# A recommender's lookup kernel whose TensorE signals its readers with a drain behind the matmul in place of the matmul itself

## The chip, the cores and the metric

The kernel runs on one core of a Trainium2 chip. The metric is device time in microseconds (us) of that core from start to end of one launch. A core has five engines that run side by side and meet only through semaphores: TensorE (PE in the profile; its weight loads are listed as PEld), VectorE (DVE), ScalarE (ACT), GpSimd (POOL) and SyncE (SP, which here only issues transfers). Matmul results go into PSUM, from which DVE and ACT read them.

## The reference

For each of 16384 rows, tables are looked up and averaged, and a small network runs over the result:

```python
tok = word_emb[token_idx].mean(axis=1)          # 32 rows of 300 floats, 50000-row table
e1 = emb_mh1[mh1_idx].mean(axis=1)              # 20 rows of 64 each, three tables
...
o1 = emb_oh1[oh1_idx]                           # one row of 64, four tables
...
emb = jnp.concatenate([tok, e1, e2, e3, o1, o2, o3, o4], axis=1)
wide = (wide_mh1[mh1_idx].sum(axis=(1, 2)) + ... + wide_oh4[oh4_idx][:, 0])[:, None]
h = jax.nn.relu(emb @ W1 + b1)                  # 748 -> 1024
h = jax.nn.relu(h @ W2 + b2)                    # -> 512
h = jax.nn.relu(h @ W3 + b3)                    # -> 256
return jax.nn.sigmoid(h @ Wd + bd + wide)
```

## The kernel before

The 16384 rows are worked through in 128 tiles of 128 rows. The large table is gathered: for each tile and each of its 32 tokens, POOL issues one indirect DMA of 128 rows of 300 floats into `tok_rows` (`gather`, L238 to L249), and DVE adds them up in `own`, a PSUM bank (`add_up`, L545). The ring `tok_rows` has three buffers of two gathers each, so up to six gathers are outstanding before POOL must wait for DVE.

The small tables are not gathered. They lie on chip as bf16 terms (`terms`), and their lookups are turned into matmuls in two moves. First, how often each table row occurs in a lookup is counted: DVE compares keys with a running index and writes one-hot rows into `hot` (`one_hots`, L619; two buffers), ACT scales half of them in place, TensorE multiplies them into a PSUM bank `pc` (`counts`, L636; two banks), and ACT copies the counts to `cnt`. Each tile takes 11 such steps of up to six matmuls, so there are 128 x 11 = 1408 steps. Second, TensorE multiplies the counts of the tile before with `terms` into the one PSUM bank `pg` (`small_sums`, L659), 138 matmuls a tile in four groups, and DVE reduces each group into the features `g`, 128 x 4 = 512 reductions. As `pg` has no second bank, the next group starts when the reduction is done.

Once features of a few tiles (four, at the end two and one) are complete, they are transposed by TensorE into `pc`, scaled by DVE into `x`, and the network's layers run in f32 (`layer`, L782): matmuls into one of two banks `ph`, each output read by ACT into `odd` or `even`.

The order of work on each engine is written by the main loop (`for step in range(n_steps)`, L948): in each step one-hots for the step after, this step's `pc` matmuls, a share of the `pg` matmuls, token gathers and adds by a pace, and a share of the layers' matmuls. So TensorE's queue holds, in turn, short bf16 matmuls for `pc` and `pg` and long f32 ones for `ph`.

A recording layer sets the waits. Every operation is recorded with what it reads and writes (`Program.record`); where another engine's operation must come first, that one is marked `signals` (L205), and only marked operations increment their engine's semaphore. Operations of TensorE never wait for TensorE. `Program.emit` (L251) then issues everything in the recorded order. All engine operations are issued from the call on L98, so nearly all rows of the profile carry that line, and tile names tell them apart. On TensorE the marked operation is the last matmul of a group whose PSUM bank is read next, or whose operands are overwritten next.

Of the kernel before, what the change touches and what calls it, by code (L numbers as in the profile page):

```python
# [71 lines left out]
class Instruction:  # L72
# [3 lines left out]
    def __init__(self, emit, sequencer, stream):  # L76
        self.emit, self.sequencer, self.stream = emit, sequencer, stream
        self.signals = False
        self.batch = [self]
# [24 lines left out]
class Program:  # L104
# [54 lines left out]
    def covers(one, other):  # L159
        return not one[0] or one[0] == other[0] and one[1] <= other[1] and other[2] <= one[2]  # L160

    def record(self, emit, sequencer, stream, reads, writes, clear=(), batch=None):
        ins = Instruction(emit, sequencer, self.stream(stream))
        if batch is not None:
# [86 lines left out]
    def emit(self, last):  # L251
        semaphores = {}
        counts = [0] * len(self.in_order)

        def semaphore(s):
            if s not in semaphores:
                name = next(n for n, k in self.streams.items() if k == s)
                semaphores[s] = self.tc.alloc_semaphore(f"sem_{name}")
            return semaphores[s]

        for s, ordered in enumerate(self.in_order):
            if any(not ordered or i.signals for i in self.members[s]):
                semaphore(s)

        def wait(engine, waits):
            for k in range(0, len(waits), 2):
                ins = engine.wait_ge(semaphore(waits[k].stream), waits[k].value)
                for o in waits[k + 1 : k + 2]:
                    ins.wait_op(semaphore(o.stream), o.value, "sem-ge")

        with self.tc.tile_critical():
            for ins in self.program:
                engine, waits = self.engines[ins.sequencer], ins.waits
                wait(engine, waits[1:])
                made = ins.emit()
                for o in waits[:1]:
                    made.wait_op(semaphore(o.stream), o.value, "sem-ge")
                s = ins.stream
                if not self.in_order[s]:
                    counts[s] += 16  # L280
                    made.then_inc(semaphore(s), 16)
                elif ins.signals:
                    counts[s] += 1
                    made.then_inc(semaphore(s), 1)
                ins.value = counts[s]
                assert counts[s] < 32768
            wait(self.engines["SP"], last)
# [13 lines left out]
class Banks:  # L301
# [8 lines left out]
    def next(self):  # L310
        if not self.free:
            self.flush()
        bank = self.free.pop(0)
        self.program.taken[bank.tensor.name] = (self, bank)
        return bank
# [756 lines left out]
```

## Time and profile before

| what | value |
|---|---|
| median of 2 runs | 6938.59 us (6930.11 to 6947.07) |
| the profiled execution, span from first to last instruction | 6960.3 us |
| ACT busy / DVE busy / POOL busy | 39% / 51% / 56% |
| TensorE busy | 79% |
| mean granted TensorE clock | 0.882 |
| mean DMA rate | 94 GB/s |
| gathers | 4096, 629.41 MB in 196608 packets |

The profile was taken of one further execution; its span is 21.7 us above the median of the two timed runs. Starts of matmuls in it are recorded, their ends are modelled. A wait is put down to the instruction whose semaphore update came last; "issue" is idle time in which an engine waited for nothing that the profile shows, and "remote" a release for which no instruction that updates that semaphore ended shortly before. A row of the timeline has start, length, engine, line, operation, tiles and count, and in brackets the idle time ahead of it and what ended that.

### The profile page before, as it was taken

To read this page: it belongs to the slowest core of one execution; us is meant where nothing else is said; L and a number is where in the kernel's file an instruction comes from. 1 tells how busy PE (TensorE), PEld (TensorE's weight loads), DVE (VectorE), ACT (ScalarE), POOL (GpSimd) and SP (SyncE) were. 2 spreads that over 40 slices of the span, in tenths; PEclk is the share of its full clock that TensorE was granted. 3 is DMA by queue.
4 is the path that set the end of the run, shared out by engine and by line. 5 is a ranking of instruction groups with operands and counts; after the bars stand their busy time and mean duration, and the time that the engine had idled before them with its cause. 6 is when DMAs were issued, how large, how long until landed. Compare 5 with 4: busy or idle time off the path is not lost.

```text
span 6960.3 us, 83647 instructions
## 1 busy us (share of the span) xinstructions
PE 5506.1 (79%) x33626; PEld 3546.0 (51%) x33626; DVE 3573.8 (51%) x6612; ACT 2697.5 (39%) x3433; POOL 3880.1 (56%) x4103
## 2 busy tenths in 40 slices
PE   5588878788788788887888787887778887878887
PEld 3455455455455545554555555544444554545666
DVE  4555555555555555555555555555555555555441
ACT  4343433333333343343343343333333333434331
POOL 6555555555555555555555555555555555555553
PEclk8788988988888998889889888898888988988898
DMA  5333333333333333333333333333333333333331
GB/s 157 95 93 94 94 94 93 92 95 93 93 96 93 94 93 93 93 95 94 93 94 94 92 94 92 95 90 90 94 92 92 92 94 92 94 92 93 89 92 50
DMA packets 253069, 651.40 MB, mean 94 GB/s; under 512 B 119195, under 2 KB 119835, under 8 KB 252679
## 3 DMA queue, kind: packets, MB, share of 16 engines
q0 software_dynamic: 196608, 629.41, 33.0%
q1 hardware_dynamic: 56071, 16.65, 1.0%
q8 instruction: 262, 4.29, 0.2%
q14 instruction: 128, 1.05, 0.0%
HBM read 645.59 MB, written 0.07 MB: 93 GB/s over the span
## 4 chain that ended last, share of the span: by engine, by line
PE 45%; another core or an unknown queue 19%; DVE 16%; issue 13%; ACT 3%; DMA 2%; POOL 2%; DVEq 0%; ACTq 0%; SPq 0%
PE ph L98 22%; PE pg L98 16%; DVE own L98 8%; PE pc L98 7%; DVE hot L98 6%; DMA tok_rows<-in_word_emb_dram,it 2%; DVE g L98 2%; POOL tok_rows L242 2%; ACT hot L98 1%; ACT cnt L98 1%; DVE x L98 0%; ACT odd L98 0%; ACT terms L98 0%; DVE wide L98 0%
## 5 line engine op out<-in xcount | busy, mean ns | idle before, releaser
L242 POOL DMA_INDIRECT tok_rows<-in_word_emb_dram,it x4096 | 3879.2, 947 | 2999.6 <-DVE own L98 1887.7
L98 PE MATMUL pg<-terms,cnt 128*128 128x195 bf16 x17664 | 2051.5, 267 | 966.2 <-DVE g L98 532.1
L98 PEld LDWEIGHTS pg<-terms,cnt 128*128 128x128 fp8e3 x17664 | 1656.3, 105 | 1229.3 <-DVE g L98 620.2
L98 DVE TENSOR_TENSOR own<-own,tok_rows 128x300 f32<-128x300 f32 x3712 | 1764.4, 475 | 477.6 <-DMA tok_rows<-in_word_emb_dram,it 363.5
L98 ACT ACTIVATE cnt<-pc 128x828 uint16<-128x828 f32 (+1 forms) x1408 | 1187.7, 844 | 2010.6 <-remote 1107.4
L98 DVE TENSOR_TENSOR hot<-own,sc 128x1656 bf16<-128x1656 bf16 (+1 forms) x1408 | 1388.4, 986 | 814.0 <-remote 474.2
L98 ACT ACTIVATE hot<-hot 64x768 bf16<-64x768 bf16 (+1 forms) x1408 | 1155.2, 820 | 1638.9 <-DVE hot L98 1434.6
L98 PE MATMUL ph<-x,w_sb 128*128 128x512 f32 (+5 forms) x3492 | 1604.8, 591 | 65.6 <-issue 43.6
L98 PEld LDWEIGHTS pc<-hot 128*128 128x128 bf16 x8192 | 630.4, 103 | 1025.6 <-issue 784.4
L98 PE MATMUL ph<-odd,w_sb 128*128 128x512 f32 (+2 forms) x2368 | 1088.6, 588 | 54.4 <-issue 51.3
L98 DVE TENSOR_REDUCE g<-pg 128x130 f32<-128x390 f32 (+1 forms) x512 | 260.7, 509 | 1469.1 <-remote 921.2
L98 PE MATMUL pc<-hot 128*128 128x138 bf16 x8192 | 804.3, 234 | 249.8 <-issue 115.1
L98 PEld LDWEIGHTS ph<-x,w_sb 128*128 128x128 f32 (+1 forms) x3492 | 639.6, 207 | 513.3 <-issue 477.4
L98 PEld LDWEIGHTS ph<-odd,w_sb 128*128 128x128 f32 x2368 | 427.9, 207 | 335.0 <-issue 324.6
L98 ACT ACTIVATE odd<-ph,b_sb 128x512 f32<-128x512 f32 (+2 forms) x365 | 231.1, 633 | 206.8 <-remote 91.7
L98 PE MATMUL ph<-even,w_sb 128*128 128x512 f32 (+2 forms) x592 | 278.3, 601 | 8.8 <-issue 8.6
L98 DVE COPY sc<-pc 128x512 bf16<-128x512 bf16 x64 | 44.2, 690 | 343.6 <-PE pc L98 191.7
L98 DVE TENSOR_TENSOR x<-pc,scale 128x768 f32<-128x768 f32 x127 | 120.7, 950 | 155.4 <-PE pc L98 84.5
L98 ACT ACTIVATE even<-ph,b_sb 128x512 f32<-128x512 f32 (+2 forms) x148 | 93.2, 630 | 224.5 <-remote 113.2
L98 PEld LDWEIGHTS ph<-even,w_sb 128*128 128x128 f32 x592 | 111.5, 211 | 92.8 <-issue 87.0
L98 PE MATMUL pc<-ident,g 128*128 128x128 f32 x762 | 115.4, 289 | 45.3 <-ACT cnt L98 26.7
L98 PEld LDWEIGHTS pc<-ident,g 128*128 128x128 f32 x762 | 87.8, 148 | 54.5 <-ACT cnt L98 31.1
(50 smaller groups left out, 547.9 us busy)
## 6 DMA issues: line engine op xcount, KB each, us to landing
tok_rows<-in_word_emb_dram,it POOLq DMA_INDIRECT x4096
ix<-in_idx_dram SPq DMA_DIRECT2D x64, 64.0 KB
w_sb<-in_W_dram SPq DMA_DIRECT2D x6, 512.0 KB
it<-in_idx_dram SPq DMA_DIRECT2D x64, 32.0 KB
w_sb<-in_W_dram SPq DMA_DIRECT2D x1, 2048.0 KB
odd<-in_mh_dram SPq DMA_DIRECT2D x3, 682.5 KB
even<-in_mh_dram SPq DMA_DIRECT2D x1, 682.5 KB
out_dram<-x SPq DMA_DIRECT2D x29, 2.0 KB
```

Source lines behind the costliest of these rows:

```text
L98: lambda: call(*args, **operands), self.name, self.name, aps + list(named.values()), outs
L242: return self.nc.gpsimd.indirect_dma_start(out=out, out_offset=None, in_=table, in_offset=bass.IndirectOffsetOnAxis(ap=index, axis=0),)
```

## The change

Where an operation of TensorE is marked as one that others wait for, `emit` now issues a further instruction of TensorE, a drain, behind it, and hangs the increment on the drain. The matmul itself no longer updates a semaphore. Values, waits and the order of all other instructions stay; on the other engines nothing differs.

```diff
@@ -281,6 +281,8 @@
                     made.then_inc(semaphore(s), 16)
                 elif ins.signals:
                     counts[s] += 1
+                    if ins.sequencer == "PE":
+                        made = self.nc.tensor.drain()
                     made.then_inc(semaphore(s), 1)
                 ins.value = counts[s]
                 assert counts[s] < 32768
```

The wait of the marked matmul was set before this point, so it stays on the matmul. Line numbers of what follows L283 rise by two.

## The prediction

> **What bounds the kernel now.** I read the page first (engines, slices, the chain that ended last), then the view of all instructions of line 98, where every operation is recorded, with the causes that ended its idle time, then the list of waits, then the timeline at two places.
>
> ```profile
> PE 5506.1 (79%) x33626; PEld 3546.0 (51%) x33626; DVE 3573.8 (51%) x6612; ACT 2697.5 (39%) x3433; POOL 3880.1 (56%) x4103
> DMA  5333333333333333333333333333333333333331
> PE 45%; another core or an unknown queue 19%; DVE 16%; issue 13%; ACT 3%; DMA 2%; POOL 2%; DVEq 0%; ACTq 0%; SPq 0%
> ```
>
> TensorE (PE) is busy 5506 of 6960 us, so it stands idle for 1454 us. The chain gives 45% of the span to PE and 19%, 0.19 x 6960 = 1322 us, to "another core or an unknown queue", though the program has one core. Which waits are those?
>
> ```profile
>   remote: 3010.1, 531
> ...
> ACT cnt L98 <- remote: 1107.4, 198, 10.3
> DVE g L98 <- remote: 921.2, 146, 7.4
> DVE hot L98 <- remote: 474.2, 101, 7.9
> ```
>
> The columns are total us and times, and in the last three rows the longest. Waits called "remote" sum to 3010 us in 531 pieces, 5.7 us each. The tiles that carry them are read out of PSUM banks that only TensorE writes (cnt<-pc, g<-pg), or wait for TensorE to be done with a buffer (hot). The view puts down a release as remote where no updating instruction ended shortly before it. So they look like increments of TensorE's semaphore that come long after the matmul. The clearest place is near the end:
>
> ```profile
> 6853.31 0.94 POOL L242 DMA_INDIRECT tok_rows<-in_word_emb_dram,it  x1 [18.84 <-DVE own L98]
> 6856.93 0.37 ACT L98 ACTIVATE odd<-ph,b_sb 128x128 f32<-128x128 f32 x1 [1.70 <-PE ph L98]
> 6860.45 0.37 ACT L98 ACTIVATE odd<-ph,b_sb 128x128 f32<-128x128 f32 x1 [3.16 <-remote]
> 6860.88 2.27 PE L98 MATMUL ph<-odd,w_sb 128*128 128x128 f32 x18 [1.08 <-ACT odd L98]
> 6879.56 0.95 POOL L242 DMA_INDIRECT tok_rows<-in_word_emb_dram,it  x1 [0.30 <-issue]
> 6881.70 0.37 ACT L98 ACTIVATE even<-ph,b_sb 128x128 f32<-128x128 f32 x1 [20.88 <-remote]
> 6882.12 1.22 PE L98 MATMUL ph<-odd,w_sb 128*128 128x128 f32 x4 [18.97 <-issue]
> ```
>
> The 18 matmuls from 6860.88 are through at 6863.15 by the profile. The ScalarE read that waits for the first layer output among them starts at 6881.70, and PE stands idle 18.97 us for that. In between nothing runs but POOL's gathers of token rows, every 1.25 us until 6879.56, and VectorE's adds of those rows. The signal comes about 1.2 us after the last gather instruction ended (6880.51). The reads at the start of that burst, up to 6856.93, were still prompt. So the trace says: while gathers stream, TensorE's completions are told late, and they come when the stream pauses. Two windows of the middle show what else happens then:
>
> ```profile
> 2995.00:3005.00 10.00, 10.00 (x80) 7.22 (x79) 4.96 (x11) 3.42 (x4) 6.80 (x8) 0.97 0.40 108
> 3020.00:3027.00 7.00, 0.73 (x8) 0.49 (x5) 0.45 (x2) 0.16 (x1) 3.49 (x4) 0.71 0.39 111
> ```
>
> Columns: length, busy us (and instructions) of PE, PEld, DVE, ACT, POOL, then clock, DMA share, GB/s. In the first window PE works through; in the second PE, DVE and ACT do next to nothing for 7 us with gathers under way. PE is the bound while it has work, and late completions are the bound when it has run out. Being told late does not stop PE at once: it goes on with whatever waits for nobody. That run-ahead is what the change touches.
>
> **The change, part by part.** The increment is taken off the matmul and put on a drain behind it; no other instruction moves. The PSUM tiles' readers give the number of drains: one signalling matmul for each.
>
> ```profile
> L98 ACT ACTIVATE cnt<-pc x1408: 621/861/902, 8.8 to 6758.7; 128x828 uint16<-128x828 f32 x160, 128x552 uint16<-128x552 f32 x16
> L98 DVE TENSOR_REDUCE g<-pg x512: 349/562/567, 85.1 to 6815.3; 128x130 f32<-128x390 f32 x128, 128x65 f32<-128x195 f32 x43
> L98 ACT ACTIVATE odd<-ph,b_sb 128x512 f32<-128x512 f32 (+2 forms) x365 | 231.1, 633 | 206.8 <-remote 91.7 <-PE ph L98 81.5 <-PE pg L98 16.9
> ```
>
> 1408 + 512 + 365 are three of the groups; the others (even 148, x 127 + 2 + 37, sc 64, terms 40, odd from pc and pg 5) bring 423, together 2708 drains, 1.9 in each of the kernel's 1408 steps. The trace of before has no drain of this sort, so its price is bounded.
>
> First price, the refill. Today the next matmul enters while the signalling one is still in the array; behind a drain it can't. How much overlap is lost is read from merged rows:
>
> ```profile
> 2996.33 0.53 PE L98 MATMUL pc<-hot 128*128 128x138 bf16 x6
> 2996.69 1.63 PE L98 MATMUL pg<-terms,cnt 128*128 128x195 bf16 x17
> 2984.68 1.02 PE L98 MATMUL ph<-odd,w_sb 128*128 128x512 f32 x2 [0.31 <-issue]
> L98 PE MATMUL pc<-hot x8192: 220/223/322, 7.9 to 6758.4; 128*128 128x138 bf16 x200
> L98 PE MATMUL pg<-terms,cnt x17664: 244/248/373, 82.4 to 6815.0; 128*128 128x195 bf16 x199
> L98 PE MATMUL ph<-odd,w_sb x2368: 275/592/1220, 420.1 to 6952.3; 128*128 128x512 f32 x155, 128*128 128x128 f32 x22, 128*128 128x256 f32 x21
> L98 PEld LDWEIGHTS pc<-hot x8192: 95/97/207, 7.9 to 6758.3; 128*128 128x128 bf16 x200
> L98 PEld LDWEIGHTS ph<-odd,w_sb x2368: 186/190/338, 420.0 to 6952.2; 128*128 128x128 f32 x198
> ```
>
> (minimum, median, maximum ns in the last five.) Six pc matmuls take 0.53 us and one 0.223, so they start (0.53 - 0.223) / 5 = 0.061 apart: each overlaps the next by 0.162. For pg it is 0.248 - (1.63 - 0.248) / 16 = 0.162, for the layers 0.592 - (1.02 - 0.592) = 0.164. At least 0.162 us is lost a drain; at most also the weight load that is hidden today, 0.097 for the 1920 drains of pc and pg and 0.190 for the other 788, so 0.29 in the mean. I take the middle, 0.23. It counts where PE had something to go on with: its matmuls wait for another engine some 310 times (179 for DVE g, 78 for ACT cnt, 34 for ACT hot, a few others), so 2708 - 310 = 2398 drains x 0.23 = 551 us (388 to 695).
>
> The TensorE page of the Trainium skill ("TensorE: Matmul & The Clock Gate", step-by-step section) says a lone matmul can't hide the emptying of the array while a stream of them does, some 166 ns at full clock. By that, 2398 x 0.166 = 398 us, an estimate; the rows' 0.162 agrees, without the reload.
>
> Second price, the run-ahead. If the drain waits until the late completions are in, PE stands still for each signal that is late, where today it works on.
>
> ```profile
> PE pg L98 <- DVE g L98: 532.1, 179, 7.9
> PE pc L98 <- ACT cnt L98: 122.9, 78, 7.4
> PE pc L98 <- ACT hot L98: 38.4, 34, 3.2
> ```
>
> Remote waits come to 3010 us on two engines and PE idles for 1454, most of it behind those same waits (532 + 123 + 38 in the rows above, and issue). So at most 3010 - 1454 = 1556 us of PE's work is done today inside them (less where DVE and ACT wait at the same time), and would be pushed out behind them. At the least it is nothing, or negative, if lateness shrinks. It should shrink: PE puts no further instructions behind an untold one, and a signal early in a burst of gathers is prompt (6856.93 above), the later one not. Between all of it and none of it I take half, 1505 us, as PE idle time. The burst above supports it no closer than that: four reads were prompt, two were late.
>
> What then still keeps PE idle without lateness: 179 waits for the reduce x 0.51 us (the page's mean) = 91 us.
>
> Sum against the profiled span: 5506 busy + 1505 late + 551 refill + 91 = 7653 us. The span of 6960.3 is 22 us above the median of the two runs, 6938.6, so 7630 us is forecast, 10% slower. Off PE the change costs nothing: POOL's gathers need 4096 x 1.25 = 5120 us, DVE 3574, ACT 2697, all with room; a drain's own message adds to the wait of each reader, but a reader that waits late already waits for microseconds.
>
> **Rivals.** (a) The drain is told at once. The drain's increment comes from the sequencer and might not stand in whatever queue holds the matmuls' completions. Then lateness is gone: 5506 + 551 + 91 - 22 = 6126 us; by the chain, 6939 - 1322 + 551 = 6168. About 6150 us, faster by 11%. For it: VectorE's adds and semaphores go on undisturbed in the burst above, so it is TensorE's path alone that is held. Against it: a drain that is to mean anything must see the matmuls complete, and what is held looks like the completion. It decides where less than (6939 - 6126) / 3010 = 27% of the lateness stays.
>
> The PSUM page of the skill ("PSUM — Partial Sum Buffer", engine vs sequencer instructions) wants the increment on the matmul, since that fires at completion, and says that a drain waits for the engine to be fully idle. By the first half of that rule nothing is late today but the work itself; by the second the drain inherits the delay, as in my forecast. This trace shows a matmul's message 18 us after its modelled end, which the first half does not lead one to expect.
>
> (b) All lateness stays, each piece now with PE idle: 5506 + 3010 + 695 + 91 - 22 = 9280 us. For it: the 18.97 us above, where nothing but the end of the gathers brought release. Against: early signals of a burst are prompt.
>
> (c) It cancels: lateness falls to about 27%, and refills eat the gain: 6800 to 7077 us.
>
> **How the numbers follow.** The forecast (30 to 80% of the lateness stays, 7029 to 8534 us) gets 0.58, (b) 0.14, (c) 0.10, (a) 0.18. About 2% is what a measurement of this kernel can tell from no change. Slower by over 2%: 0.58 + 0.14 = 0.72; within 2%: 0.10; faster: 0.18. The range goes from the lower edge of (c), 6800, to just over (b), 9300, and leaves out (a) and little else; the forecast's own is 7029 to 8534.
>
> **What would show it.** In the profile after: PE's busy time about as before, its idle time up from 1454 to over 2000 us; remote waits of ACT and DVE replaced by waits on PE's sequencer or on drains; after each signal at least 0.16 us more between matmuls; no PE work inside a late wait. If (a) is right, the 19% of the chain goes to nearly nothing and PE's busy share rises towards 90%. I am wrong if TensorE's signals become prompt while gathers stream, or if the refill is several times 0.23 us because a drain itself takes long.

## The result, and the profile after

| | kernel before | changed kernel |
|---|---|---|
| median of 2 runs | 6938.59 us | 7715.26 us (7701.54 to 7728.99) |
| profiled execution: span | 6960.3 us | 7727.1 us |

The changed kernel is slower by a ratio of 1.1115 (95% interval 1.1088 to 1.1142), 777 us. The forecast was 7630 us.

Here are the engines, and the chain that ended last by engine, from the page of the changed kernel:

```profile
PE 5804.2 (75%) x33626; PEld 3547.7 (46%) x33626; DVE 3610.5 (47%) x6612; ACT 2716.9 (35%) x3433; POOL 3890.1 (50%) x4103
issue 46%; PEld 33%; PEldq 11%; DVE 6%; ACT 3%; DMA 0%; SPq 0%; POOL 0%; DVEq 0%
```

"PEldq" is TensorE's sequencer, where drains are listed. The "another core or an unknown queue" of before is gone from the chain, but not the time: TensorE idles 7727 - 5804 = 1923 us, where it was 1454. From the view of line 98, with the causes that ended idle time, and from the view of the drains' own line 285:

```profile
  PEq L285: 6874.7, 2332
...
L285 PEldq DRAIN  x2709: 13/2272/19290, 4.9 to 7721.6; - x194
```

The first of these rows says that other engines stood 6875 us, in 2332 waits, until a drain ended; there is no "remote" row left. The second gives minimum, median and maximum ns of a drain, from when the sequencer reaches it until it is done, so most of it is the time of matmuls ahead of it that are still to be done. Who stands there is in the view of waits of the changed kernel (us in total, times, longest us):

```profile
POOL tok_rows L242 <- DVE own L98: 2571.9, 936, 19.4
ACT cnt L98 <- PEq L285: 2389.3, 974, 9.6
DVE g L98 <- PEq L285: 1782.4, 385, 10.1
...
DVE hot L98 <- PEq L285: 1154.8, 492, 9.6
...
ACT even L98 <- PEq L285: 281.8, 105, 19.4
```

The readers of all three kinds of PSUM tile (`cnt` from `pc`, `g` from `pg`, `even` from `ph`) wait for drains, and POOL, which issues the gathers, waits for VectorE behind them: every engine is behind TensorE.

What counts is how long a drain goes on behind the modelled end of its last matmul. Taken from the trace for all 2709: 2034 end within 0.15 us of it, most of them 0.021 us behind, and 675 are late, with 1668 us in sum. One of these is in the timeline of the changed kernel:

```profile
3006.60 0.53 PE L98 MATMUL pc<-hot 128*128 128x138 bf16 x6
3007.30 1.55 PE L98 MATMUL pg<-terms,cnt 128*128 128x195 bf16 x16 [0.18 <-issue]
3010.20 0.56 DVE L98 TENSOR_REDUCE g<-pg 128x130 f32<-128x390 f32 x1 [4.67 <-PEq L285]
3010.22 1.12 PE L98 MATMUL ph<-x,w_sb 128*128 128x512 f32 x2 [1.37 <-issue]
```

The pg matmuls end at 3008.85. The reduction that waits for their drain starts at 3010.20, and so does TensorE's next matmul, which waits for nobody but the drain. Before, TensorE would have gone on at once. The 0.18 us ahead of the pg row is a drain that isn't late, seen as a gap between two matmul groups: it ends 0.117 us behind its matmul, and the next matmul starts 0.059 us later.

### The profile page after: what moved, and what is told of

Same layout as the page of the kernel before. It is cut to its first block, busy times and chain, and to the rows that moved or that the text cites. A ratio compares the mean times of both kernels' runs of the same rounds, so it can differ in the third digit from the quotient of the medians.

```text
span 7727.1 us, 86356 instructions
## 1 busy us (share of the span) xinstructions
PE 5804.2 (75%) x33626; PEld 3547.7 (46%) x33626; DVE 3610.5 (47%) x6612; ACT 2716.9 (35%) x3433; POOL 3890.1 (50%) x4103
## 4 chain that ended last, share of the span: by engine, by line
issue 46%; PEld 33%; PEldq 11%; DVE 6%; ACT 3%; DMA 0%; SPq 0%; POOL 0%; DVEq 0%
PEld pg L98 16%; PEldq L285 11%; PEld ph L98 10%; PEld pc L98 7%; DVE hot L98 3%; ACT hot L98 2%; DVE own L98 2%; ACT cnt L98 0%; DVE g L98 0%; SPq L238 0%; DMA tok_rows<-in_word_emb_dram,it 0%; POOL tok_rows L242 0%; ACT x L98 0%; DMA it<-in_idx_dram 0%; DVE x L98 0%
## 5 line engine op out<-in xcount | busy, mean ns | idle before, releaser
L98 PE MATMUL pg<-terms,cnt 128*128 128x195 bf16 x17664 | 2021.1, 273 | 1216.1 <-issue 1144.4
L98 PE MATMUL ph<-x,w_sb 128*128 128x512 f32 (+5 forms) x3492 | 1638.1, 594 | 203.9 <-issue 159.4
L98 PEld LDWEIGHTS pc<-hot 128*128 128x128 bf16 x8192 | 596.9, 101 | 999.2 <-issue 883.2
L98 PEld LDWEIGHTS ph<-x,w_sb 128*128 128x128 f32 (+1 forms) x3492 | 618.5, 204 | 762.9 <-issue 741.7
L98 PE MATMUL pc<-hot 128*128 128x138 bf16 x8192 | 762.6, 230 | 211.5 <-issue 166.9
```

Source lines behind the costliest of these rows:

```text
L98: lambda: call(*args, **operands), self.name, self.name, aps + list(named.values()), outs
```

## The experiments

There are twelve experiments, in four sets, and each set also timed the kernel before. It took 5212 to 5225 us there, not 6939: something about the first pair of runs was different, and it was not the kernel. Comparisons below are within a set where nothing else is said.

**The kernel before, unchanged, for its trace.** No edit.

> The kernel before, unchanged, for a trace under the conditions of the study. If its time is about 5225 us: remote waits below 100 us (3010 us in the first trace), TensorE busy above 90% of the span. Ratio 1.00.

Measured: 5212.61 us, ratio 1.0 (0.9991 to 1.001). From its page, the engines and the chain that ended last:

```profile
PE 4861.1 (93%) x33626; PEld 3267.3 (63%) x33626; DVE 3577.5 (69%) x6612; ACT 2685.7 (52%) x3433; POOL 3875.1 (74%) x4103
POOL 32%; DMA 31%; issue 15%; DVE 14%; PE 8%; ACT 0%; DVEq 0%; POOLq 0%; SPq 0%
```

No wait at all is put down as remote. Of 358 waits that an update of TensorE's semaphore ended, each ended 16 ns or less behind the matmul's modelled end; in the first trace it was 1444 waits with a median of 2273 ns. Of the 1750 us between the two spans, 1105 are idle time of TensorE and 645 are busy time. And the bound is another one: POOL and the DMA of the gathers carry 63% of the chain, TensorE 8%. The view of waits of this run names the same:

```profile
DVE own L98 <- DMA tok_rows<-in_word_emb_dram,it: 1395.3, 1385, 6.7
POOL tok_rows L242 <- issue: 773.5, 2522, 2.0
POOL tok_rows L242 <- DVE own L98: 464.5, 1457, 4.0
```

VectorE stands 1395 us until gathered rows have landed, and POOL waits only 465 us for VectorE to free a buffer, so the gathers are late and not their readers.

**The changed kernel, twice more.** No edit.

> The changed kernel once more, beside the kernel before, since in the first runs of the study the kernel before took 5225 us in place of 6939. If late completions are a condition of where or when a kernel runs, and the refill is a cost of the drain itself: where the kernel before takes about 5225 us, the changed kernel takes 5600 to 5700 us (ratio 1.07 to 1.09), and where it takes about 6940, 7715 (ratio 1.11). If the increment on the drain has a cost of its own beside the drain's stop: above 5750 us.

> The changed kernel a third time, to see whether the conditions of the first pair (kernel before at 6939 us, late completions) come back. Theory: ratio 1.11 if the kernel before takes about 6940 us, 1.07 if it takes about 5215, whatever else differs. If the ratio of 1.11 appeared at 5215 us as well, lateness would not be what separates the two.

Measured: 5581.83 us, ratio 1.0706 (1.0688 to 1.0724), and 5582.75 us, ratio 1.071 (1.0692 to 1.0728). Of 2709 drains none ended more than 0.15 us behind its matmul. The engines and the chain of the first of the two, from its page:

```profile
PE 5266.0 (94%) x33626; PEld 3224.8 (58%) x33626; DVE 3604.5 (65%) x6612; ACT 2707.7 (49%) x3433; POOL 3877.9 (70%) x4103
...
PEld 36%; issue 30%; PEldq 12%; DVE 11%; DMA 4%; POOL 3%; ACT 3%; DVEq 0%; SPq 0%
```

POOL and DMA have 7% of the chain in place of 63%: TensorE's queue (weight loads, their issue, the drains) has become the longest path. TensorE's busy time is up from 4861 to 5266 us, and its idle time is down from 349 to 313 us. The time of the first repetition is 18 us under the 5600 us that its expectation began at; the ratio is inside. So the change loses 7% without any lateness, and 11% with it. The conditions of the first pair did not come back.

**Drain and signal taken apart**, twice.

The cut is against the kernel before.

```diff
                     counts[s] += 1
                     made.then_inc(semaphore(s), 1)
+                    if ins.sequencer == "PE":
+                        self.nc.tensor.drain()
```

> The drain stands behind each signalling matmul, but the increment stays on the matmul, so a reader need not wait for the drain's own message. Theory (TensorE stands still at each drain until its completions are in): the same time as the changed kernel, 7600 to 7800 us. Rival (readers are told later because the message comes from the drain and not from the matmul): near the time of before, 6900 to 7050 us.

> The drain behind each signalling matmul with the increment left on the matmul, once more, beside the changed kernel in the same runs. Theory: within 1.5% of it at about 5215 us for the kernel before (5641 against 5582 was measured in different runs: 1.1% more), and also where completions are late, since TensorE stands still in both. If it is over 2% faster than the changed kernel where completions are late, the readers gain by hearing from the matmul.

Measured: 5641.18 us, ratio 1.0794 (1.0776 to 1.0812), and 5641.12 us, ratio 1.0823 (1.0805 to 1.0841), against 5582.75 us for the changed kernel in the set of the second. The times in us of the first expectation rested on 6939 us for the kernel before and can't be met; as ratios they come to 1.095 to 1.124 for the theory and at most 1.016 for the rival, and 1.079 is in neither. What holds is the comparison with the changed kernel, within the 1.5% of the second expectation. With readers told by the matmul, the whole loss stays, so where completions are prompt it comes from TensorE's stop and not from where the message is sent. It is even 58 us more: these drains end 0.047 us behind the matmul in place of 0.021, and 2709 x 0.026 = 70 us. Whether readers gain by the matmul's message where completions are late wasn't seen.

**The gathers left out, without and with drains.** The adds read zeroed buffers; the token part of the features is left out.

```diff
-                    program.gather(f"gather{tokp.slot}", rows[-1], word, it[:, j : j + 1], batch, tok_rows)
...
+    for rows in tokp.all:
+        nc.vector.memset(rows, 0.0)
```

> The kernel before without the 4096 gathers of token rows (the adds read buffers that are zeroed once; the token part of the features is left out). Theory (TensorE's completions are told late only while gathers stream): remote waits all but gone, TensorE the bound, 5550 to 5900 us. Rival (completions are late by TensorE's own load): remote waits stay in the thousands of us, time above 6500.

> The changed kernel without the gathers, as in the run before it. Theory: the drains then cost the refill alone, 450 to 650 us above the same kernel without drains, and drains that end more than 0.15 us behind their matmul sum to less than 100 us (1668 us with gathers). Rival (a drain is slow by itself): the difference is above 800 us.

Measured: 4810.86 us and 5529.8 us, one run each. The engines of the one, then of the other, from their pages:

```profile
PE 4740.6 (99%) x33626; PEld 3251.6 (68%) x33626; DVE 3563.4 (74%) x6615; ACT 2697.6 (56%) x3433; POOL 0.9 (0%) x7
```

```profile
PE 5256.5 (95%) x33626; PEld 3218.5 (58%) x33626; DVE 3594.6 (65%) x6615; ACT 2710.6 (49%) x3433; POOL 0.9 (0%) x7
```

The first expectation failed on its time, 739 us under its lowest: it reckoned from the first pair. No wait is put down as remote and TensorE is the bound, as it said. It is in both runs, so the difference is the bare price of the drains: 719 us, 0.265 us each. It lies about half way between the theory's upper bound (650) and the rival's lower one (800), so both failed. TensorE's busy time grows by 516 us, 0.190 a drain: matmuls that overlapped now stand one behind the other. Compared matmul by matmul, the two traces give the parts: the signalling matmul overlapped the next one by 423 us in sum, 0.156 each, and with drains by nothing; and the matmul behind a drain takes 97 us longer in sum, 0.036 each, most where it is an f32 one. The TensorE page of the Trainium skill ("TensorE: Matmul & The Clock Gate", step-by-step section) says that a lone matmul can't hide the emptying of the array and a stream does; its section "Single matmul latency" puts at 166 ns what a lone matmul at full clock pays beside its columns, issue included. The 0.156 agrees with that, but as ends of matmuls are modelled, this split rests on the model; the 0.265 us in sum is measured time. TensorE's idle time grows by 203 us, 0.075 a drain, of which the trace shows two parts: the drain ends 0.021 us behind the matmul's modelled end, and the next instruction starts 0.052 us later. That gathers are what makes completions late is not shown by this pair, because in the same set completions were prompt with gathers too.

**Two drains in place of one.**

```diff
+                        self.nc.tensor.drain()
                         made = self.nc.tensor.drain()
```

> The changed kernel with a second drain behind each drain (2709 more); the second finds TensorE empty. Theory (what a drain costs is the emptied array and the restart, not the instruction): 0.01 to 0.06 us for each further drain, 30 to 160 us above the changed kernel (5582 us where the kernel before takes 5214), so 5610 to 5740 us. Rival (a drain costs its 0.265 us as an instruction): 700 us more, near 6300.

Measured: 5782.26 us, ratio 1.1068 (1.105 to 1.1086). Against 5582 us, in another set, that is 200 us for 2709 further drains, 0.074 us each. It is just outside the expected 0.01 to 0.06 us, far from the rival's 0.265, and the same as the 0.075 us above. So a drain costs 0.075 us as an instruction, and 0.19 us because matmuls no longer overlap across it.

**Drains behind some of the matmuls only.** The cut is against the changed kernel; an operation also keeps the name of the tile that it writes.

```diff
-                    if ins.sequencer == "PE":
+                    if ins.sequencer == "PE" and ins.tile.startswith("pc"):
```

> Drains behind the 1604 signalling matmuls that write pc alone; the other 1105 signal by themselves. Theory (each drain costs the same refill wherever it stands): 1604 / 2709 = 59% of the changed kernel's loss, ratio 1.040 to 1.055. Rival (what counts is run-ahead, which TensorE has most of behind the pc matmuls): over 80% of the loss, ratio above 1.063.

> The complement: drains behind the 1105 signalling matmuls that write pg or ph. Theory: 41% of the loss, ratio 1.025 to 1.040, and the losses of this kernel and of the one with drains behind pc alone add up to that of the changed kernel within 60 us. Rival: under 20% of the loss, ratio below 1.016.

Measured: 5285.68 us, ratio 1.0136 (1.0119 to 1.0153), and, with `not` ahead of the second condition, 5227.76 us, ratio 1.0025 (1.0015 to 1.0035). Together they lose 72 + 14 = 86 us, and both at once lose 368. The theory fails in both, and so does the rival of the first; the second lies below its rival's bound of 1.016, but not for its reason. The loss is neither shared by number nor lies behind the pc matmuls. The chains that ended last, first of the kernel with drains behind pc, then of the other, give the reason:

```profile
PE 77%; issue 6%; DVE 6%; DMA 4%; POOL 4%; PEld 2%; PEldq 1%; ACT 0%; DVEq 0%; SPq 0%
```

```profile
DMA 23%; POOL 23%; PE 19%; issue 14%; DVE 12%; PEld 7%; PEldq 1%; ACT 1%; DVEq 0%; SPq 0%; POOLq 0%
```

The kernel before runs at the pace of the gathers, and TensorE's own path is shorter. TensorE's path with n drains, 4811 + 0.265 n by the set without gathers, comes to 5104 us for the 1105 drains, still under the 5214 us of the gathers; to 5236 for the 1604, just over; and to 5530 for all. Measured were 5228, 5286 and 5582. The first 400 us of drains are hidden, and what comes behind them counts in full: from 1604 drains to all the time grows by 296 us, and 1105 x 0.265 is 293. The 50 us by which the last two stand above this sum are not explained.

**Half of the gathers left out** in the kernel before, to test that. The buffers are zeroed as above.

```diff
-                    program.gather(f"gather{tokp.slot}", rows[-1], word, it[:, j : j + 1], batch, tok_rows)
+                    if r == 0:
+                        program.gather(f"gather{tokp.slot}", rows[-1], word, it[:, j : j + 1], batch, tok_rows)
```

> The kernel before with one gather of each pair left out (2048 in place of 4096; the other half of the buffer stays zero and half the token part of the features is left out). Theory (in the runs of the study the kernel before is bound by the stream of gathers, 4096 x 1.25 us, and TensorE's own path is some 4800 us): the time falls to 4800 to 4900 us, near the 4811 us without any gather. Rival (gather traffic slows TensorE itself, so that the time falls in proportion): about 5010 us, half way between 5214 and 4811.

Measured: 4818.58 us, ratio 0.9224 (0.9208 to 0.9239), inside the theory's 4800 to 4900 us and 8 us from the kernel with no gathers, which ran in another set. Its chain is TensorE's own, from the page of this run:

```profile
PE 4739.7 (98%) x33626; PEld 3251.5 (68%) x33626; DVE 3569.1 (74%) x6615; ACT 2696.9 (56%) x3433; POOL 1947.8 (40%) x2055
...
PE 96%; DVE 2%; ACT 1%; DMA 1%; issue 0%; POOL 0%; DVEq 0%; POOLq 0%; SPq 0%
```

Half of the gathers cost TensorE nothing; the whole stream is a bound of its own.

**Narrow gathers in the changed kernel.** Rows of 75 floats of the table seen as rows of that width; the buffers are zeroed as above.

```diff
-                    program.gather(f"gather{tokp.slot}", rows[-1], word, it[:, j : j + 1], batch, tok_rows)
+                    program.gather(f"gather{tokp.slot}", rows[-1][:, 0:75], word.rearrange("v (a d) -> (v a) d", d=75), it[:, j : j + 1], batch, tok_rows)
```

> The changed kernel with gathers of 75 floats a row in place of 300 (a quarter of the bytes and as many gathers and rows; the token part of the features is not the reference's). If the bytes of the gathers hold TensorE's completions, late drains sum to some 400 to 700 us in place of 1668 and the time falls to 6300 to 6800 us. If it is the issuing by POOL or the number of rows, late drains stay at 1300 to 1900 us and the time at 7300 to 7750.

Measured: 5577.79 us, one run, with no late drain at all; the changed kernel with full rows takes 5582 in another set. The queue of the gathers (packets, MB, share of 16 engines' span), here and then in the first repetition of the changed kernel:

```profile
q0 software_dynamic: 131072, 157.55, 16.4%
```

```profile
q0 software_dynamic: 196608, 629.41, 41.6%
```

A quarter of the bytes is moved, and the time is the same. As no drain was late with full rows either, the run answers nothing about lateness, and neither of its two expected times came. It shows that the bytes of the gathers do not bear on the 5582 us.

## Why the prediction was right

The forecast named 7630 us and slower; 7715 was measured, for the forecast's own reason: TensorE stands still for completions that come late, and pays the refill besides. The closeness of the number is luck in part, since the largest term was a choice and the terms were off in opposite directions.

- Number of drains: 2708 were worked out, there are 2709.
- Late time that becomes TensorE's idle time: 1505 us forecast as half of 3010, 1668 measured on the drains. The half was a choice between bounds and came near by no finer reason.
- Refill: 551 us forecast, 0.23 each on 2398. In the changed kernel's first trace TensorE's busy time is up by 298 us, drains that aren't late add 1713 - 1668 = 45 us of idle time (1713 us is TensorE's idle time inside all drains), and 2709 restarts of 0.053 us 143, 486 in all. By itself a drain costs 0.265 us, near the upper bound of 0.29, but made up otherwise: the forecast's upper bound had a hidden weight load of 0.12 us in the mean in it, where 0.036 came, and 0.075 us lie on the drain itself, which the working left at nothing.
- Other idle time: 91 us forecast. Of the 210 us of idle time outside drains, 143 are those restarts; 67 are left.
- With these, 5506 + 1668 + 486 + 67 = 7727 us, the span, which is split here and so comes out by itself. Against the forecast's 7653 us of span, the late term came out 163 us higher, and the other two 65 and 24 us lower.
- Rival (a), the drain is told at once: refuted where completions are late, since 675 drains waited for them. The PSUM page of the Trainium skill ("PSUM — Partial Sum Buffer", engine vs sequencer instructions) has a drain wait until the engine is fully idle. These drains agree: of the 2709, none ended ahead of its matmul's modelled end.
- Rival (b), all lateness stays: 1668 of 3010 us did. Rival (c), it cancels: not so, the interval of the ratio begins at 1.1088.
- What was to be seen: idle time over 2000 us was forecast, 1923 came. "PE's busy time about as before" was wrong by 298 us, since a matmul that no longer overlaps the next one counts as busy for longer.
- "While gathers stream, TensorE's completions are told late" holds within the first pair only. In the trace of the changed kernel, 5 of 1042 drains were late where at most two gathers had started in the 6 us ahead of the matmul's end, and 619 of 1179 where four or more had; of the 50 drains behind the last gather none was. But in the first repetition 2427 drains had four or more gathers ahead of them, and none was late. So lateness went with gathers under way, and they alone do not make it.
- "Off PE the change costs nothing" held. But the prediction took the first trace's bound for the kernel's. In the sets of the study the kernel before is bound by gathers, and a price per drain does not add up there. The ratio is then 1.07, and the forecast of 1.10 would have been too high.

What stays open is why TensorE's completions were told late in the first pair. The first trace of before holds 2457 updates of TensorE's semaphore for 2709 signalling matmuls, and 19614 of the three gather semaphores; the trace of the same kernel from the study holds 2708 and 65478. Records were lost in the first, and next to none in the second. VectorE's updates were lost as well, 4594 recorded against 6210, and none of the 1000 of its messages that could be followed was late, so lost records alone do not go with late messages. Whether recording held up TensorE's completions, or both have another cause, was not tried, as the condition did not come back.

## What to carry to other kernels

Leave the increment on the matmul: a drain behind it costs TensorE a quarter of a microsecond for lost overlap and a restart, and it gives away the work that TensorE does while a reader is not yet told. The price counts only once TensorE's path is the longest, so find the bound first; here the first 400 us were free. And when a wait has no visible releaser, run the same kernel a second time on another occasion before a change is built on it: 1700 us of the first time were not the kernel's.

## What the runs showed of the hardware that was not expected

The same program took 6939 us on one occasion and 5212 to 5225 us on four others. On the first, completions of TensorE came up to 21 us late, while VectorE's semaphore updates came 12 ns behind the instruction or less, in all 1000 waits of ScalarE that they ended in that trace. TensorE ran on meanwhile, but not without end: in the 1444 waits above, never more than 62 later instructions (weight loads and matmuls) had started behind a matmul when its message came.

The granted clock also differed: 0.882 with late completions, 0.98 without. The trace holds two values of it, 1 and 0.5, in 262 stretches each on the first occasion and 36 on the later one. In the 4 us ahead of a stretch at 0.5, TensorE was idle for 67% of the time in the mean, and over the whole span for 21%. At 0.5 the pg matmuls started 0.164 us apart, at full clock 0.087. As 1210 us of TensorE's busy time fell into such stretches, against 161 us later, some 500 of the 645 us of further busy time are the clock's, by an estimate from these figures.
